# Layer 3 of a four-layer attention and feed-forward stack: when the feed-forward weights are prepared, and who copies the first turned tokens

## The chip, the core and the metric

The kernel runs on one core of a Trainium2 chip. A core has a matrix engine (TensorE, PE in the profile, with its weight loads as PEld), a vector engine (VectorE, DVE), an activation engine (ScalarE, ACT), a general engine (GpSimd, POOL) and a queue that only issues transfers (SyncE, SP). Each engine works through its own instructions in order, and waits on semaphores for the others. The metric is the device time of one execution in microseconds; lower is better.

## The reference

Four layers, each an attention block and a feed-forward block with a residual sum, on x of 4 batches x 256 tokens x 256 features, with a context of 4 x 1601 x 256. The change is in the last layer:

```python
# x = x + _L3_xattn_ref(_layernorm(x), ctx_2048, Wq, Wk, Wv)
q = x @ Wq.T
k_raw = context @ Wk.T
v_raw = context @ Wv.T
...            # 32 heads of 8 features; q and k get an rms norm over the 8
scores = jnp.einsum('bhnd,bhmd->bhnm', q, k) * scale
attn = jax.nn.softmax(scores, axis=-1)
out = jnp.einsum('bhnm,bhmd->bhnd', attn, v)

# x = x + _L3_ffn_ref(_layernorm(x), w_gate, w_up, w_down)
def _quant_weight(w):
    scale = jnp.mean(jnp.abs(w)) + EPS
    wq = jnp.clip(jnp.round(w / scale), -1.0, 1.0)
    return (wq, scale)
...            # activations are rounded to 8 bits with a scale for each token
gate = jax.nn.silu(_qlinear(x, w_gate))
up = _qlinear(x, w_up)
return _qlinear(gate * up, w_down)
```

The three feed-forward weights (each 256 x 1024 values) are thus loaded, summed in absolute value over all elements, and rounded to -1, 0 or 1 before any token can use them.

## The kernel before, in words

The kernel computes the layers one after the other; layer 3 (method `l3`) is its last fifth. Its heart is a loop of 208 **slots**: 4 batches x 4 groups of heads x 13 blocks of 128 context rows (`m`). In each slot the program issues, in this order:

- `scores`: 8 score products on TensorE (`s<-qb,kb`) into one of three PSUM tiles, and two exponentials on ScalarE (`e<-s`);
- at certain `m` a fixed extra. At the first slot of each part (`m` = 0, 3, 6, 9): the casts of the next part's keys on GpSimd (`kb<-kf`) and the loads of the part after that on SP (`kf<-kd`, 8 transfers). At `m` = 2: `close` of the group before (4 transposes, then VectorE divides). At `m` = 7: `asked`, first part (the next group's queries are split in two halves, VectorE and GpSimd). At `m` = 9: `asked`, second part: two transposes on TensorE (`b<-ident,halfq`) whose result VectorE shuffles into `row`;
- one call of `slot`, which hands out background work;
- `values` of the slot before (`o<-e,va`, 4 products). After a group's last block VectorE copies the sum out (`os<-o`), and the next group's first product into the single tile `o` has to wait for that copy. For `m` = 0 the call of `slot` comes after this.

**Background work** is written as streams: Python generators that issue some instructions and then yield. A yield of `True` means that the next piece needs TensorE and the shared PSUM tile `b`. A yield of a number is the VectorE time in microseconds that the author reckons for the next piece, 0.0 if there is next to none. `slot` serves at most one wanting stream (the one with the lowest count of pieces served for its share; none at `m` = 2 and `m` = 9), and gives every other stream at most one piece: the longest-waiting costed piece first, whatever it costs, and then others as long as they fit the room (1.7 in most slots, 1.1 at `m` = 0, 0.8 where the fixed extra took TensorE, 0.5 more if no wanting piece was served). So a yield of 0.0 is a step that holds a stream back for one slot. Nothing in this order depends on run time: all engines are pinned to program order from the first slot on (`self.strict`, lines 2353 to 2355). Because of that pinning the profile gives line L77, a helper, for nearly all instructions of the loop; they are told apart by their tiles.

The streams of batch 0 are

- `weights` (lines 2099 to 2134): for each of the three weights two loads of 512 KB on GpSimd's queue (`wf<-in_l_wg` and so on, into the two buffers of the tag `g3`), two absolute row sums on VectorE (`wsum<-wf`), one product with a matrix of ones (`b<-wsum,ones`, called here the product of the row sums), three small VectorE operations, and six rounding passes on VectorE;
- `ahead` (line 2289): mean and variance of batches 1 to 3, their inverse roots (`root3n`), and then `queries(1)`: normalised tokens (`xn`), 4 transposes into `b`, a copy to `xT`, 8 products, a copy to `qr`, squares and roots;
- `every` (line 2357, the keys) and `l3_values`: the products of the next batch's context that are still missing (`b<-wkv,ctx`, each copied out by VectorE), then from the moment that batch 1's keys have been sent those of batch 2;
- `l3_spread`: root, scaling (`kr<-kr,ss`, GpSimd), splitting (`half`, VectorE and GpSimd), turning (`kt<-half`, VectorE) and sending (`kd<-kt`, 4 transfers on SP) of batch 1's keys to memory, from where `kf` loads them.

In each later batch, `half` (line 2305) runs the feed-forward block of the batch before; it begins when all three weights are ready and the tokens are normalised (`behind`).

`bank()` is the shared PSUM tile `b`. Its pool has one buffer, so a new user waits on TensorE until the reader of the last one (mostly VectorE) has finished.

Before the loop, `queries(0)` (line 2059) runs the same steps for batch 0, without yields that matter, mixed with `fill`: products of batch 1's context (`fill<-wkv,ctx`) whose copies and squares are on ScalarE.

Of the kernel before, what the change touches and what calls it, by code (L numbers as in the profile page):

```python
# [97 lines left out]
class Kernel:  # L98
# [79 lines left out]
    def fill(self, n):  # L178

        for _ in range(n):  # L180
            next(self.early, None)
# [1828 lines left out]
    def l3(self, first):  # L2010
# [9 lines left out]
        nc, tc, i = self.nc, self.tc, self.i  # L2020
        with ExitStack() as es:
# [10 lines left out]
            def bank():  # L2032
                return ps.tile([P, 512], F32, name="b3", tag="tp")
# [9 lines left out]
            def normed(b, r):  # L2043
                xn = self.xn.tile([P, 2, D], F32, name="xn3", tag="xn")
                for q in range(2):
                    nc.vector.tensor_scalar(
                        xn[:, q, :], self.x[b][:, q, :], mv[:, b, q, 0:1], r[:, q : q + 1], ALU.subtract, ALU.mult
                    )
                return xn
# [9 lines left out]
            def queries(b, st, fill=lambda n: None):  # L2059

                xn = normed(b, rs[:, b, :])
                fill(0)
                if b:
                    yield 0.0
                yield True
                tp = bank().rearrange("p (k q t) -> p k q t", k=2, q=2)
                for k in range(2):
                    for q in range(2):  # L2070
                        self.ordered(nc.tensor.transpose(tp[:, k, q, :], xn[:, q, k * P : (k + 1) * P], self.ident))
                xT = one.tile([P, 2, S], F32, name="xT3")
                nc.vector.tensor_copy(xT, tp.rearrange("p k q t -> p k (q t)"))
                fill(1)
                yield 0.0
                yield True
                tq = bank().rearrange("p (q d) -> p q d", q=2)
                for q in range(2):
                    for k in range(2):
                        self.mm(tq[:, q, :], xT[:, k, q * P : (q + 1) * P], self.wq3[:, k, :], k == 0, k == 1)  # L2080
                qr = two.tile([P, 2, D], F32, name="qr3")
                nc.vector.tensor_copy(qr, tq)
                yield 0.8
                ss = one.tile([P, 2 * NH3], F32, name="ssq3")
                for q in range(2):
                    self.l3_squares(ss, qr[:, q : q + 1, :], q, True, two)
                yield 0.8
                if b:
                    yield from self.roots(ss, ss, 1.0 / HD3, 1e-6, two.tile([P, 1, D], F32, name="sqq3")[:, 0, :])
                    yield 0.6  # L2090
                else:
                    self.rstd(ss, ss, 1.0 / HD3, self.eps6)
                qrv = qr.rearrange("p q (h d) -> p (q h) d", d=HD3)
                nc.vector.tensor_tensor(qrv, qrv, ss[:, :, None].to_broadcast([P, 2 * NH3, HD3]), ALU.mult)
                fill(2)
                st["qr"] = qr
                yield 0.0

            def weights():

                for name, n in (("l3_wg", 2), ("l3_wu", 2), ("l3_wd", 8)):
                    v = i[name].rearrange("(k p) e -> p k e", p=P)
                    w = []
                    for c in range(2):
                        w.append(two.tile([P, I3], F32, name="wf3", tag="g3"))
                        nc.gpsimd.dma_start(
                            w[c].rearrange("p (k e) -> p k e", k=n // 2), v[:, c * n // 2 : (c + 1) * n // 2]
                        )
                    for _ in range(2):
                        yield 0.0  # L2110
                    sm = self.small.tile([P, 2], F32, name="wsum")
                    for c in range(2):
                        yield 1.2
                        nc.vector.tensor_reduce(sm[:, c : c + 1], w[c], AX.X, ALU.add, apply_absolute_value=True)
                    yield 0.0
                    yield True
                    tot = bank()[:, 0:2]
                    self.mm(tot, self.ones, sm, True, True)
                    s = one.tile([P, 1], F32, name=name + "s")
                    r = self.small.tile([P, 1], F32, name="wrec")  # L2120
                    nc.vector.tensor_reduce(s, tot, AX.X, ALU.add)
                    nc.vector.tensor_scalar(s, s, 1.0 / (I3 * D), 1e-5, ALU.mult, ALU.add)
                    nc.vector.reciprocal(r, s)
                    wb = one.tile([P, n, 2048 // n], BF16, name=name + "b")
                    wr = wb.rearrange("p k e -> p (k e)")
                    for c in range(2):
                        yield 0.8
                        nc.vector.tensor_scalar(w[c], w[c], r, RND, ALU.mult, ALU.add)
                        yield 0.7
                        nc.vector.tensor_scalar(w[c], w[c], RND, 1.0, ALU.subtract, ALU.min)  # L2130
                        yield 0.7
                        nc.vector.tensor_scalar(wr[:, c * I3 : (c + 1) * I3], w[c], -1.0, None, ALU.max)
                    wq[name], ws[name] = wb, s
                    yield 0.0
# [154 lines left out]
            def ahead(b, st):  # L2289

                if b == 1:
                    yield from norms()
                    yield 1.0
                yield from queries(b, st)
# [46 lines left out]
            for _ in queries(0, first, lambda n: [next(kv) for _ in range(FIRST3[n])]):  # L2341
                pass
# [3 lines left out]
            q = next(ask)  # L2346
# [7 lines left out]
            whole, nc = nc, InOrder(nc, self.pin)  # L2354
# [4 lines left out]
            for at, (b, g, c) in enumerate(order):  # L2359
                if g + c == 0:  # L2360
                    streams = [t for t in streams if t.left] if b else [Stream(weights(), 3)]
                    st = states[b + 1] if b + 1 < B else None
                    if b + 1 < B:
                        every.n, every.share = 0, K3[b]
                        if b == 0:
                            streams += [every, Stream(self.l3_spreads(states), 1)]
# [3 lines left out]
                k, m0 = k1, PARTS[c][0]  # L2370
                for m in range(*PARTS[c]):
# [13 lines left out]
                    if m == 7 and (g < 3 or b + 1 < B):  # L2385
# [4 lines left out]
                        q = next(ask)  # L2390
# [30 lines left out]
            def wide(dt=F32):  # L2421
                return ps_s.tile([P, 1024 if dt is F32 else 2048], dt, name="w3", tag="s3")
# [7 lines left out]
            b = B - 1  # L2430
# [6 lines left out]
            for q in range(2):  # L2437
# [8 lines left out]
                tp = wide(BF16)[:, : 2 * P].rearrange("p (k t) -> p k t", k=2)  # L2446
                for k in range(2):
                    self.ordered(nc.tensor.transpose(tp[:, k, :], vb[:, k * P : (k + 1) * P], idb))
                xT = two.tile([P, 2, P], BF16, name="xqT3")
# [217 lines left out]
```

## Time and profile before

| | |
|---|---|
| median of 3 runs | 2333.57 us |
| the runs | 2330.38, 2333.57, 2341.16 us |
| the profiled execution: its own time | 2349.27 us |
| its span, first to last instruction | 2347.5 us |
| mean granted TensorE clock in it | 0.984 |
| start of the first slot, batch 0 | 1860.43 us |
| start of slot 0 in batches 1, 2 and 3 | 1985.44, 2103.38, 2216.63 us |
| start of the last slot of batch 3 | 2315.62 us |

The profile is of one execution, which took 15.7 us more than the median of the runs. A slot is read from it as the distance between the starts of two score products (`s<-qb,kb`) on TensorE. Where nothing is late a slot takes 1.83 us without background work on TensorE (two exponentials bound it) and 2.50 us with one context product; 2.02 us with a `close`, some 3.3 us with the 8 query products. The undisturbed length is the same all through the loop, so a longer slot shows a wait or a slowed clock.

### The profile page before, as it was taken

The page shows a single profiled execution, that of the slowest core. Times are in us where ns is not written, and L with a number is a line of the kernel's source. Part 1 is how long each engine was busy: PE and PEld are TensorE (multiplying, and loading weights), DVE is VectorE, ACT ScalarE, POOL GpSimd, SP SyncE. Part 2 cuts the span into 40 slices and gives each one's busy share as a digit, 9 for nine tenths or more (in the row PEclk, how much of TensorE's full clock was granted, in tenths as well). Part 3 has the DMA queues.
Part 4 walks back from the last instruction along what each step waited for, and adds up shares of the span by engine and source line. Part 5 has one row for each costly group of instructions (what it writes and reads, how often), then busy time and mean ns, then how long its engine had stood idle before and what let it go on. Part 6 is the DMA issues. An engine that isn't in the chain of part 4 may idle for free.

```text
span 2347.5 us, 42368 instructions
## 1 busy us (share of the span) xinstructions
PE 2251.9 (96%) x14381; PEld 1381.1 (59%) x14395; DVE 1462.6 (62%) x3534; ACT 1270.3 (54%) x2884; POOL 950.3 (40%) x1723
## 2 busy tenths in 40 slices
PE   8999999889989999999999999999999989999997
PEld 5677878767745565555655555555765633343332
DVE  5553535863557777877787778877334474748343
ACT  3334445533565544455555555554332487888996
POOL 2014654513345455544555445554221253434220
PEclk9999999899999999999999999999899999999999
DMA  7165576743631111111111111100434353434220
GB/s 272 42 207 167 171 152 187 234 129 91 193 135 43 52 52 52 42 48 45 50 57 52 52 52 52 49 9 10 196 125 119 114 157 107 108 98 106 80 69 18
DMA packets 157166, 234.47 MB, mean 100 GB/s; under 512 B 33993, under 2 KB 122825, under 8 KB 155754
## 3 DMA queue, kind: packets, MB, share of 16 engines
q1 hardware_dynamic: 140902, 190.86, 25.3%
q0 software_dynamic: 11280, 31.60, 5.4%
q10 hardware_dynamic: 4772, 9.31, 1.2%
q8 instruction: 118, 1.93, 0.3%
q14 instruction: 94, 0.77, 0.1%
HBM read 169.94 MB, written 61.74 MB: 99 GB/s over the span
## 4 chain that ended last, share of the span: by engine, by line
PE 81%; DVE 8%; DMA 4%; ACT 2%; issue 2%; POOL 1%; SPq 1%; ACTq 0%; another core or an unknown queue 0%; DVEq 0%; POOLq 0%
PE o L117 18%; PE s L117 17%; PE o L77 7%; PE b L77 4%; PE f2gu L117 3%; PE s L77 3%; PE fill L1353 3%; PE acc L117 2%; PE f1gu L117 2%; PE f0gu L117 2%; PE tpq L117 2%; PE av L117 2%; PE f0y L117 2%; PE f2y L117 1%; DMA f0xr<-f0xd,f0src 1%
## 5 line engine op out<-in xcount | busy, mean ns | idle before, releaser
L1618 ACT ACTIVATE p<-s,nmsm 128x448 f32<-128x448 f32 (+2 forms) x512 | 324.3, 638 | 388.0 <-DVE nmsm L1613 316.3
L117 PE MATMUL o<-pT,va 128*128 128x256 f32 (+2 forms) x1920 | 431.6, 377 | 0.2
L117 PE MATMUL s<-kT,qT 128*32 128x448 f32 (+2 forms) x4096 | 424.2, 550 | 4.2 <-ACT p L1618 4.2
L77 ACT ACTIVATE e<-s 128x1024 f32<-128x1024 f32 (+1 forms) x416 | 393.1, 1040 | 56.3 <-PE s L77 54.3
L117 PEld LDWEIGHTS o<-pT,va 128*128 128x128 f32 (+1 forms) x1920 | 344.8, 190 | 124.3 <-issue 72.5
L1656 POOL TENSOR_SCALAR p<-p,rm 128x416 f32<-128x416 f32 x508 | 316.9, 645 | 6.3
L1613 DVE TENSOR_REDUCE nmsm<-s 128x1 f32<-128x448 f32 (+4 forms) x384 | 292.8, 783 | 4.2
L1662 DVE STREAM_TRANSPOSE pT<-p 128x448 f32<-128x448 f32 (+4 forms) x384 | 277.8, 777 | 9.7 <-POOL p L1656 9.7
L117 PEld LDWEIGHTS s<-kT,qT 128*32 128x32 f32 x4096 | 121.7, 109 | 250.2 <-issue 213.9
L77 PE MATMUL o<-e,va 128*32 128x512 f32 (+1 forms) x1664 | 249.6, 613 | 5.8 <-DVE os L77 4.1
L1646 POOL TENSOR_TENSOR rm<-em,tot 32x8 f32<-32x8 f32 x256 | 49.9, 195 | 337.1 <-DVE tot L1643 306.9
L77 PEld LDWEIGHTS s<-qb,kb 32*128 32x128 f32 (+1 forms) x1664 | 65.8, 181 | 177.2 <-issue 134.3
L1610 DVE TENSOR_TENSOR s<-s,mask 128x64 f32<-128x64 f32 (+4 forms) x384 | 92.2, 259 | 124.9 <-PE s L117 75.0
L1353 PE MATMUL fill<-wkc_early,ctxT 128*128 128x256 f32 (+1 forms) x444 | 109.6, 399 | 10.1 <-ACT va_early L1361 8.3
L545 POOL DMA_INDIRECT f0xr<-f0xd,f0src x95 | 90.9, 956 | 68.0 <-PE f0y L117 18.0
L77 PE MATMUL s<-qb,kb 32*128 32x256 f32 (+1 forms) x1664 | 111.8, 332 | 4.2 <-POOL kb L77 1.3
L1353 PEld LDWEIGHTS fill<-wkc_early,ctxT 128*128 128x128 f32 (+1 forms) x444 | 86.3, 198 | 28.0 <-ACT va_early L1361 10.4
L1618 ACT ACTIVATION_READ_ACCUMULATOR p<-s,nmsm 128x1 f32 x512 | 100.5, 196 | 0.0
L77 POOL CAST kb<-kf 128x384 fp32r<-128x384 f32 (+1 forms) x126 | 64.4, 540 | 88.2 <-PE s L77 29.8
L117 PE MATMUL f2gu<-f2wgu,f2xsT 128*128 x176 | 84.6, 605 | 0.6 <-ACT f2xsT L114 0.3
L77 PEld LDWEIGHTS o<-e,va 128*32 128x32 f32 (+1 forms) x1664 | 41.6, 108 | 68.5 <-issue 35.9
L655 POOL DMA_INDIRECT f0yt<-f0yd,f0slot x64 | 66.9, 1045 | 35.7 <-DMA kd<-kT_early 16.4
(570 smaller groups left out, 3669.1 us busy)
## 6 DMA issues: line engine op xcount, KB each, us to landing
kf<-kd SPq DMA_DIRECT2D x384, 48.0 KB
vd<-va_early SPq DMA_DIRECT2D x96, 128.0 KB
kd<-kT_early SPq DMA_DIRECT2D x48, 256.0 KB
kT<-kd SPq DMA_DIRECT2D x16, 768.0 KB
va<-vd SPq DMA_DIRECT2D x16, 768.0 KB
kd<-kt SPq DMA_DIRECT2D x96, 128.0 KB
f0yd<-f0ys SPq DMA_DIRECT2D x95, 128.0 KB
ctxT<-in_ctxT SPq DMA_DIRECT2D x5, 1664.0 KB
```

The lines of the kernel that those rows point to most:

```text
L77: ins = f(*a, **kw)
L117: self.ordered(self.nc.tensor.matmul(out, lhsT, rhs, start=start, stop=stop, **kw))
L545: nc.gpsimd.indirect_dma_start(out=t, out_offset=None, in_=xd[:, :], in_offset=bass.IndirectOffsetOnAxis(ap=src[:, n : n + 1], axis=0),)
L655: self.pin(nc.gpsimd.indirect_dma_start(out=yt, out_offset=None, in_=yd[:, :], in_offset=bass.IndirectOffsetOnAxis(ap=slot[:, t, r : r + 1 ...
L1353: ins = nc.tensor.matmul(tp[:rows, t, :], ctxT[u // NKV2][:, k, c0 : c0 + rows], w[u % NKV2][:, k, :], start=k == 0, stop=k == 1,)
L1610: nc.vector.tensor_tensor(sv, sv, mask[:, e0:e1, : nt - CT, :].rearrange("p n t i -> p n (t i)"), ALU.add)
L1613: nc.vector.tensor_reduce(ms[:, 0, e0:e1], s[:, n0:n1, : nt * 32], AX.X, ALU.max, negate=True)
L1618: nc.scalar.activation(p[:, n, : nt * 32], s[:, n, : nt * 32], AF.Exp, bias=ms[:, 0, e : e + 1], accum_out=ms[:, 1, e : e + 1],)
L1646: nc.gpsimd.tensor_tensor(r[32 * a : 32 * a + 32], e[:, a], tot, ALU.mult)
L1656: nc.gpsimd.tensor_scalar(p[:, n, : nt * 32], p[:, n, : nt * 32], r[:, e : e + 1], 1.0, ALU.mult, ALU.mult)
L1662: self.pin(nc.vector.transpose(pT[:, 2 * c + n0 : 2 * c + n1, :nt, :].rearrange("p n t i -> p n (t i)"), p[:, n0:n1, : nt * 32],))
```

## The change

Three edits, all in `l3`.

1. For batch 0 alone (`b` is 0), the copy of the turned tokens to `xT`, ahead of the loop, is issued on ScalarE (`nc.scalar.copy`) and no longer on VectorE.
2. The `weights` stream begins with twelve steps of 0.0, so its first load is issued twelve slots later.
3. Behind the two row sums of each of the three weights stand four steps of 0.0 where there was one, ahead of the piece that issues the product of the row sums.

No instruction is added or dropped; one changes its engine, and the slots of most background pieces of batches 0 to 2 change with the order.

```diff
@@ -2070,7 +2070,7 @@
                 xT = one.tile([P, 2, S], F32, name="xT3")
-                nc.vector.tensor_copy(xT, tp.rearrange("p k q t -> p k (q t)"))
+                (nc.vector.tensor_copy if b else nc.scalar.copy)(xT, tp.rearrange("p k q t -> p k (q t)"))
                 fill(1)
@@ -2098,6 +2098,8 @@
             def weights():
 
+                for _ in range(12):
+                    yield 0.0
                 for name, n in (("l3_wg", 2), ("l3_wu", 2), ("l3_wd", 8)):
@@ -2112,7 +2114,8 @@
                     for c in range(2):
                         yield 1.2
                         nc.vector.tensor_reduce(sm[:, c : c + 1], w[c], AX.X, ALU.add, apply_absolute_value=True)
-                    yield 0.0
+                    for _ in range(4):
+                        yield 0.0
                     yield True
                     tot = bank()[:, 0:2]
                     self.mm(tot, self.ones, sm, True, True)
```

## The prediction

> **What bounds the kernel now.** I read the page first (TensorE leads), then busy time and granted clock by batch of layer 3, and then the timelines of TensorE and VectorE in batch 0.
>
> ```profile
> PE 2251.9 (96%) x14381; PEld 1381.1 (59%) x14395; DVE 1462.6 (62%) x3534; ACT 1270.3 (54%) x2884; POOL 950.3 (40%) x1723
> ...
> 1860.43:1985.44 125.01, 115.18 (x931) 45.94 (x931) 79.86 (x189) 99.30 (x107) 53.46 (x81) 0.93 0.47 133
> 1985.44:2103.38 117.94, 114.52 (x1014) 47.95 (x1014) 71.09 (x185) 101.90 (x111) 46.01 (x76) 1.00 0.42 117
> ```
>
> Columns of the stretches: length, busy PE, PEld, DVE, ACT, POOL, clock, DMA share, GB/s. Batch 0 takes 125.0 us, batch 1 takes 117.9; in batch 0 TensorE is idle for 9.8 us, and only there the mean clock is under 1. The idle time stands in a few stops:
>
> ```profile
> 1852.04 1.99 PE L117 MATMUL b<-wq,xT 128*128 128x256 f32 x8 [2.09 <-DVE xT L2073]
> ...
> 1895.20 1.27 PE L77 MATMUL o<-e,va 128*32 128x512 f32 x8 [2.57 <-DVE os L77]
> ...
> 1914.33 0.38 PE L77 MATMUL b<-wsum,ones 128*128 128x2 f32 x2 [2.90 <-DVE wsum L77]
> ...
> 1942.63 0.89 PE L77 MATMUL s<-qb,kb 32*128 32x256 f32 x8 [1.34 <-POOL kb L77]
> ```
>
> And behind the three in the loop the clock is low for 3.4 us:
>
> ```profile
> 1896.40:1899.80 3.40, 3.40 (x28) 1.50 (x24) 2.33 (x7) 1.94 (x2) 3.04 (x4) 0.57 0.84 200
> ...
> 1916.90:1920.30 3.40, 3.40 (x26) 0.91 (x24) 3.26 (x11) 1.76 (x3) 2.58 (x4) 0.57 0.31 87
> ...
> 1944.20:1947.60 3.40, 3.40 (x19) 1.45 (x17) 0.77 (x3) 2.13 (x3) 0.00 (x0) 0.57 0.35 99
> ```
>
> The first two stops have one cause: VectorE is some 4 us late all through slots 7 to 30. It copies a group's sum out late (`os`), and the row sums of the second weight stand behind other work and a transfer:
>
> ```profile
> 1887.25 0.44 DVE L77 STREAM_SHUFFLE row<-b 128x256 f32<-128x256 f32 x1
> ...
> 1894.47 0.68 DVE L77 COPY os<-o 128x512 f32<-128x512 f32 x1
> ...
> 1908.80 1.22 DVE L77 TENSOR_REDUCE wsum<-wf 128x1 f32<-128x1024 f32 x1 [0.94 <-DMA wf<-in_l_wu]
> 1936.49 1.22 DVE L77 TENSOR_REDUCE wsum<-wf 128x1 f32<-128x1024 f32 x1 [2.35 <-DMA wf<-in_l_wd]
> ```
>
> The `row` of slot 9 comes at 1887.25, though its transposes ended at 1883.3. The third stop is the same lateness passed on: SP sends turned keys only after VectorE has turned them, key loads queue behind those sends, and the casts (`kb`) wait for them.
>
> **The order after.** The slot rule fixes the order of both versions. Stepping the streams through it gives, for before, each of the trace's 208 slots with the TensorE work that it shows. The slots in which pieces are issued (batch 0 unless said):
>
> - first weight: load 0 → 12, sums 3, 5 → 15, 17, product 7 → 23, last rounding 14 → 29
> - second: load 15 → 30, sums 18, 19 → 33, 34, product 21 → 39, last rounding 27 → 47
> - third: load 28 → 48, sums 31, 33 → 51 and slot 0 of batch 1, product 45 → slot 16 of batch 1, last rounding slot 0 → 23 of batch 1
> - queries of batch 1: `xn` 11 → 8, transposes and `xT` copy 13 → 10, products 16 → 12
> - keys of batch 1: sends 10..33 → 8..28; context products of batch 2: 36..51 → 30..45
> - feed-forward of batch 0: 12..48 → 25..51 of batch 1. Batch 3 keeps its order.
>
> No slot is added, and TensorE's and ScalarE's totals stay (but for the one copy). The later products of the row sums hold back only the roundings and through them batch 0's feed-forward block, which now ends in slot 51 of batch 1; nothing waits for its result, so that costs nothing as long as its TensorE pieces find slots, which they do. What moves is lateness.
>
> **What goes.** Slot lengths less the undisturbed 1.83, 2.50 and 2.02: slots 14 and 15 (4.28, 3.32, the latter with a `close`) 2.45 + 1.30; slots 21 and 22 (4.72, 3.28) 2.89 + 1.45; slots 34, 35, 36 (3.25, 3.29, 3.01, the last with a product) 1.42 + 1.46 + 0.51; slot 49 (3.46 with a product, behind `row`) 0.96. Sum 12.4 us. Each stop costs its idle time and about 1.3 to 2 us of low clock. They go if VectorE is on time at these places. Its work in slots 13 to 19 after is 1.4, 2.5, 2.1, 3.2, 2.5, 2.2 and 1.1 us (from the rows: a row sum 1.21, a turn 1.24, a root step 1 to 1.7, a rounding pass 0.7 to 0.9), about 3 us late at slot 18, worked off by slot 23. In that time TensorE waits for VectorE only through `row` at slot 22, whose splitting is issued at slot 20, and for the product at slot 23, six slots behind its second sum. So I take all 12.4.
>
> **What comes.** (a) Slot 9's transposes leave their result in `b`, and slot 10 now wants `b` for the queries' transposes; before, four slots lay between. VectorE up to that `row` loses the two row sums (1.21 + 1.19), three small operations (0.46) and a rounding pass (0.74), 3.6 us, and gains the last root steps (0.7), one split (0.45) and `xn` (1.70), 2.9 us. So `row` ends near 1887.4 against 1888.0. TensorE stands at the transposes of slot 10 from 1884.8 (the slot's start 1884.31 + 0.44 of scores): 2.6 us, less 0.3 for a late start of slots 9 and 10 themselves, is a new stop of 2.3 us, plus 1.3 of clock: 3.6. Bounds: 1.0 (under the 1.15 us stop at 1992, behind which the clock stayed 1.00) and 4.34 (slots 21 and 22). What is queued behind: this batch's `o` and the next scores; ScalarE runs dry with them. The `os` of slot 13 then finds VectorE on time.
>
> (b) The loads. Rows: the second weight's sum began 6.5 us after its load's issue, the third's 5.3, both on landing. First weight: three slots from load to sum, one of 3.3 us, no stop. Second: three slots with products, 7.5 us; none. Third: issued behind slot 48's casts, some 2.4 us into it; lands at 7.7 where VectorE asks at 6.5; then one split, and `os` of the next slot at about 9.35 where the sum is ready at 8.8 and `o` wanted at 9.6. That is the 0.35 to 0.45 us wait that `os` has elsewhere. Cost 0; bounds -0.5 and 3.75 (slots 14 and 15). GpSimd's casts behind the loads have three slots of room; SP issues as many transfers as before.
>
> The Trainium skill (DMA: Bandwidth & Descriptors, Anatomy of one DMA) reckons 2.0 us plus bytes over 436 GB/s, an estimate of 3.2 us for 512 KB. The rows of 5.3 and 6.5 us, with the queue shared, decide; by the page (b) could not cost anything.
>
> (c) Batches 1 and 2: the feed-forward block meets root and split of batch 3's keys in slots 44 to 50 of batch 1; VectorE has 3.3 + 3.1 + 2.9 us in three slots of 2.5, 2.5 and 1.98, 2.6 us late at most; `b` is wanted at once after `row` in slot 49. I take +0.5; bounds 0 and 2.5. The long slot 22 of batch 2 (2.82) has another order: -0.5, bounds -1 and 0.
>
> (d) The `xT` copy. VectorE's copy ran 1851.30 to 1851.98, behind a reduction that waited for a ScalarE square until 1850.66. On ScalarE it follows the pair of copies that ends near 1851.1; 128x256 copies there take 0.37, so 128x512 about 0.65, done near 1851.7: -0.3. Bounds: -1.9 (first in line, at 1849.5) and +0.9 (behind the next pair and square).
>
> Sum: -12.4 + 3.6 + 0 + 0.5 - 0.5 - 0.3 = -9.1 us, on a span of 2347.5; the median is 0.6% shorter, which changes the sum by 0.1. Forecast 2324.5.
>
> A rule against this: the Trainium skill (TensorE: Matmul & The Clock Gate, HAM oscillation) asks only that no idle gap exceed about 3.4 us. By it the stops of 2.57, 2.90 and 1.34 cost no clock. The 0.57 behind each of them says otherwise here; by the rule 4.7 us of the 12.4 (1.30 + 1.45 + 1.46 + 0.51) and 1.3 of the 3.6 would not be there: -5.7.
>
> **Rivals.** *A, the stop at slot 10 is short.* For it: without a GpSimd operation beside them, root steps take 0.17 us (they took 1.0 to 1.28 with one). Against: `kr` and `half` run there after too. With 1.0 for (a) the sum is -11.7, with (d) at its best -13.3: 2320 to 2322.
>
> *B, the lateness only changes places.* (a) at 4.34, (b) at 3.75, (c) at 2.5 and 0, (d) as forecast: -2.1, 2331.5. Against: by the same sum of VectorE's work it is at most 1.7 us late in slots 23 to 50.
>
> *C, slower: the row sums stand on their loads.* VectorE waits in order; a sum that waits for its load holds `row`, the copies out of `b` and `os` behind it. The bound from the trace is the first weight's load, issued at 1862.2 beside the 1.7 MB context loads and used unhindered at 1872.8: at most 10.6 us. At 10.6 in all three places: first 3.9 (2.6 at slot 22 and the clock), second 0.5, third 6.6 (5.3 at `os` and the clock): +11.0, net +1.9, 2335.5. From some 9.9 us it is slower than before. Against: the two rows at 5.3 and 6.5.
>
> **How the numbers follow.** Two medians of this kernel differ without a change by up to about 0.5% (the three runs spread 10.8 us); 0.5% is 2321.9 or less, or 2345.2 or more. Forecast 0.51 (own range 2319.5 to 2330), A 0.23, B 0.10, C 0.10, and 0.06 for a slowdown that none of these names. Faster by over 0.5%: 0.42 of the forecast's share, for its 9.1 lies 2.6 short of the bound with that spread, and 0.83 of A: 0.41. Slower: half of C (where loads take longer still) and the unnamed: 0.11. The rest, 0.48, is within. Range 2316 to 2336: A's best and the runs' spread below, C at the top.
>
> **What would show it.** Right: no stop behind `os` at slot 14 nor behind `wsum`; batch 0 near 116 us; one stop of about 2 us at the transposes `b<-ident,xn` in slot 10, its releaser `row` on VectorE, and low clock behind it; `kb` never the releaser of a stop. Wrong: no stop there (A), `wsum` waiting for its load by over 3 us (C), or new stops of over 1.3 us in batch 1 (B).

## The result, and the profile after

The changed kernel took 2346.80 us (median of 6 runs, 2342.53 to 2349.07), the kernel before 2337.17 us beside it (6 runs, 2330.38 to 2341.16). The ratio is 1.0044, with a 95% interval of 1.0032 to 1.0055: slower by some 10 us, where 9 us less were forecast.

The profiled execution of the kernel after took 2343.73 us, that of the kernel before 2349.27 us. The two spans thus say the opposite of the medians. The loop of layer 3 does not: from its first score product to that of its last slot it went from 455.19 to 462.63 us. First the page's busy times, then the stretches of the loop's first three batches, in the columns of the prediction (length, busy PE, PEld, DVE, ACT, POOL, granted clock, DMA share, GB/s):

```profile
PE 2246.1 (96%) x14395; PEld 1379.0 (59%) x14395; DVE 1462.4 (62%) x3533; ACT 1277.2 (55%) x2885; POOL 948.2 (40%) x1723
```

```profile
1847.16:1971.69 124.53, 112.22 (x928) 44.16 (x928) 80.59 (x189) 98.82 (x107) 58.50 (x87) 0.95 0.51 140
1971.69:2097.95 126.26, 119.57 (x1026) 50.09 (x1024) 79.68 (x202) 102.91 (x111) 45.32 (x75) 0.97 0.41 106
2097.95:2210.80 112.85, 110.44 (x980) 43.68 (x976) 55.86 (x160) 100.40 (x111) 36.94 (x67) 1.00 0.37 90
```

Busy time does not show the loss; the totals are those of before. Batch 0 did not fall to 116 us but stayed at 124.5 (before: 125.0), and batch 1 grew from 117.9 to 126.3, with a clock under 1 that it did not have before. The timeline of TensorE (start, length, line, output<-inputs, idle time before and what ended it) shows where:

```profile
1871.86 0.63 PE L77 MATMUL b<-ident,xn 128*128 128x128 f32 x4 [1.94 <-DVE row L77]
...
1896.93 0.39 PE L77 MATMUL s<-qb,kb 32*128 32x256 f32 x4 [1.42 <-POOL kb L77]
...
1900.75 0.69 PE L77 MATMUL b<-ident,halfq 128*128 128x128 f32 x2 [2.72 <-POOL halfq L77]
...
1963.50 0.69 PE L77 MATMUL b<-ident,halfq 128*128 128x128 f32 x2 [1.94 <-POOL halfq L77]
...
1977.68 1.94 PE L77 MATMUL o<-e,va 128*32 128x512 f32 x8 [3.68 <-DVE os L77]
```

The first is the forecast stop of slot 10. The old stops at `os` (slot 14), `wsum` (slot 21) and `kb` (slot 34) are gone, as forecast. The other rows are new: slot 22, slot 48, and slot 1 of batch 1. The stop of slot 22 has its chain in VectorE and GpSimd. VectorE first (the turn of slot 14, the first weight's two row sums, the last root step of the keys' second part):

```profile
1884.47 1.25 DVE L77 STREAM_TRANSPOSE kt<-half 128x1024 f32<-128x1024 f32 x1 [2.45 <-DMA kf<-kd]
...
1887.70 1.21 DVE L77 TENSOR_REDUCE wsum<-wf 128x1 f32<-128x1024 f32 x1
...
1891.45 1.21 DVE L77 TENSOR_REDUCE wsum<-wf 128x1 f32<-128x1024 f32 x1
...
1894.90 0.33 DVE L77 SCALAR_TENSOR_TENSOR ss<-half 128x160 f32<-128x160 f32 x1
```

Then GpSimd, which waits for that last step:

```profile
1895.31 1.07 POOL L77 TENSOR_TENSOR kr<-kr,ss 128x512 f32<-128x512 f32 x1 [5.88 <-DVE ss L77]
1896.32 1.26 POOL L77 CAST kb<-kf 128x449 fp32r<-128x449 f32 x2
1897.54 1.70 POOL L77 TENSOR_TENSOR half<-kr,half 128x512 f32<-128x512 f32 x1
1899.21 1.07 POOL L77 TENSOR_TENSOR kr<-kr,ss 128x512 f32<-128x512 f32 x1
1900.24 0.45 POOL L77 TENSOR_TENSOR halfq<-qr,halfq 128x128 f32<-128x128 f32 x1
```

Slot 18 began at 1888.11; the scaling issued in it began 7.2 us later, and everything behind it on GpSimd, the casts `kb` and the queries' `halfq` that TensorE needs in slot 22, is late with it. In slot 48 VectorE waited for GpSimd's squares of keys (`sq`), and a rounding pass of the second weight came before the queries' split, which GpSimd's `halfq` needs:

```profile
1961.49 0.69 DVE L77 TENSOR_REDUCE ss<-sq 128x64 f32<-128x512 f32 x1 [4.10 <-POOL sq L77]
1962.10 0.68 DVE L77 TENSOR_SCALAR wf<-wf 128x1024 f32<-128x1024 f32 x1
1962.70 0.22 DVE L77 TENSOR_SCALAR halfq<-qr 128x128 uint32<-128x128 uint32 x1
```

At the start of batch 1 the same two engines stand in the way of `os`:

```profile
1973.65 1.25 DVE L77 STREAM_TRANSPOSE kt<-half 128x1024 f32<-128x1024 f32 x1 [3.94 <-POOL half L77]
1975.47 1.22 DVE L77 TENSOR_REDUCE wsum<-wf 128x1 f32<-128x1024 f32 x1 [0.58 <-DMA wf<-in_l_wd]
1976.61 0.42 DVE L77 TENSOR_SCALAR half<-kr 128x512 uint32<-128x512 uint32 x1
1976.94 0.68 DVE L77 COPY os<-o 128x512 f32<-128x512 f32 x1
```

TensorE stood from 1974.0 us on (1977.68 less 3.68); a turn that waited 3.94 us for GpSimd and a row sum of the third weight were ahead of `os` in VectorE's queue. VectorE's part of that split was done at 1969.7 us. GpSimd was late with its part (`half`) because two casts, until 1970.7, and then the third weight's load issue stood ahead of it:

```profile
1970.71 1.60 POOL L77 DMA_DIRECT2D wf<-in_l_wd  x2
1972.33 1.29 POOL L77 TENSOR_TENSOR half<-kr,half 128x512 f32<-128x512 f32 x1
```

### The profile page after: what moved, and what is told of

It is laid out like the page before. It is cut to its first block, busy times and chain, and to the rows that moved or that the text cites. A ratio compares the mean times of both kernels' runs of the same rounds, so it can differ in the third digit from the quotient of the medians.

```text
span 2341.9 us, 42389 instructions
## 1 busy us (share of the span) xinstructions
PE 2246.1 (96%) x14395; PEld 1379.0 (59%) x14395; DVE 1462.4 (62%) x3533; ACT 1277.2 (55%) x2885; POOL 948.2 (40%) x1723
## 3 DMA queue, kind: packets, MB, share of 16 engines
q8 instruction: 118, 1.93, 0.3%
## 4 chain that ended last, share of the span: by engine, by line
PE 78%; DVE 8%; DMA 5%; ACT 3%; issue 3%; POOL 2%; SPq 1%; ACTq 0%; POOLq 0%; DVEq 0%
PE o L117 18%; PE s L117 17%; PE o L77 7%; PE b L77 3%; PE f2gu L117 3%; PE s L77 3%; PE acc L117 2%; PE f0gu L117 2%; PE f1gu L117 2%; PE tpq L117 2%; PE av L117 2%; PE fill L1353 2%; PE s L329 2%; DMA f0xr<-f0xd,f0src 2%; PE f0y L117 1%
## 5 line engine op out<-in xcount | busy, mean ns | idle before, releaser
L117 PEld LDWEIGHTS o<-pT,va 128*128 128x128 f32 (+1 forms) x1920 | 344.8, 190 | 124.5 <-issue 72.5
L77 PE MATMUL s<-qb,kb 32*128 32x256 f32 (+1 forms) x1664 | 112.9, 333 | 4.4 <-POOL kb L77 1.7
L117 PE MATMUL f0gu<-f0w,f0xsT 128*128 x380 | 78.0, 327 | 1.6 <-DVE ss_early L126 1.2
```

The lines of the kernel that those rows point to most:

```text
L77: ins = f(*a, **kw)
L117: self.ordered(self.nc.tensor.matmul(out, lhsT, rhs, start=start, stop=stop, **kw))
```

## The experiments

The runs were made on several occasions, on which the kernel before had medians from 2334 to 2348 us, so each version is compared with runs of the kernel before beside it. The ratio is the one given with the result; it need not be exactly the quotient of the medians. As a second, finer measure I give the loop **from slot 4 of batch 0 to the last slot** in the profile: the first four slots differ by some 2 us between executions of one kernel, and the part ahead of the loop by over 10. Before: 442.88 us. After: 452.46 us.

### Are the profiles typical? (e5, e14)

The kernel before and the changed kernel, each profiled a second time, nothing changed.

> The kernel before, profiled a second time. Theory chance (the prediction's terms were read from one execution that stood 13 us above the median of its own kernel): the stretch from the first fill product to the first score is 22.65 us without the 2.09 us stop before the query products, and the loop of layer 3 (first score to last) is 451 to 453 us instead of 455.2. Theory structure (the stops belong to the kernel): 25.0 us and 455 us again.

> The changed kernel again, beside the two others on one chip, with a second profile. If its stops belong to the kernel: os 3.5 to 3.9 us at the start of batch 1, halfq 2.5 to 2.9 in slot 22, loop 461 to 465, time 8 to 12 us above the kernel before. If they were the chance of one execution: loop under 458, time within 5 us.

Before: 2332.17 us in its one run (2334.14 beside it); the 22.65 us from the first fill product to the first score have no stop at the query products; loop 449.69, from slot 4 439.53. TensorE's stops in it, and batch 0:

```profile
1880.62 1.06 PE L77 MATMUL o<-e,va 128*32 128x512 f32 x8 [2.66 <-DVE os L77]
1898.71 0.38 PE L77 MATMUL b<-wsum,ones 128*128 128x2 f32 x2 [1.85 <-DVE wsum L77]
1926.01 0.89 PE L77 MATMUL s<-qb,kb 32*128 32x256 f32 x8 [0.61 <-POOL kb L77]
```

```profile
1847.89:1967.32 119.43, 111.02 (x932) 44.07 (x932) 81.54 (x189) 99.29 (x107) 53.90 (x81) 0.97 0.50 140
```

The places are the same, but the stops at `wsum` and `kb` are smaller (2.90 and 1.34 us in the first profile), and the 2.09 us stop ahead of the query products is not there. So the first profile of before, 16 us above the median of the first three runs, was dearer than the kernel: 3.4 us of it in the loop from slot 4, 2.1 in the first four slots, 2.4 between the first fill product and the first score, and the rest ahead of that. The theory of chance holds, and by more than it said.

After, again: 2359.12 us against 2347.21, ratio 1.0053 (1.0034 to 1.0073); from slot 4 452.20 us (first profile 452.46); slot 22 stops 1.26 and 2.72 us, the start of batch 1 4.82 (3.5 to 3.9 were expected). The stops of after belong to the kernel.

Slot lengths above the undisturbed ones given with the profile before (a slot with the four query transposes is taken at 2.1 us), in both profiles of each (us):

| slots | before | after | the prediction's term |
|---|---|---|---|
| batch 0, 9 to 11 | 0.0, 0.0 | 2.0, 2.0 | +3.6 (a) |
| 14 to 16 | 3.8, 3.9 | 0.7, 0.7 | -3.8 |
| 21 to 25 | 4.6, 3.2 | 7.6, 7.0 | -4.3 |
| 34 to 36 | 3.4, 1.1 | 0.4, 1.4 | -3.4 |
| 48 and 49 | 0.9, 0.9 | 3.1, 1.6 | -1.0 |
| batch 1, 1 to 3 | 1.5, 1.5 | 6.1, 6.9 | 0 (b) |
| 46 to 48 | 0.0, 0.0 | 2.9, 2.9 | +0.5 (c) |
| batch 2, 1 to 4 and 22 | 1.9, 1.9 | 1.7, 1.7 | -0.5 (c) |

These places add up to 8.4 us more in the first pair of profiles and 11.7 in the second, of the 9.6 and 12.7 us by which the loop from slot 4 grew.

### The parts of the change one by one (e1, e2, e3)

```diff
-                nc.vector.tensor_copy(xT, ...)                                   # e1 alone
+                (nc.vector.tensor_copy if b else nc.scalar.copy)(xT, ...)
+                for _ in range(12):                                              # e2 alone
+                    yield 0.0
-                    yield 0.0                                                    # e3 alone
+                    for _ in range(4):
+                        yield 0.0
```

> Kernel before with the first edit alone (xT copied by ScalarE for batch 0). The trace of after has 22.65 us from the first fill product to the first score, before has 25.01. If the copy alone does that, this kernel has no stop before the 8 query products and is 2 to 2.5 us faster than before (0.1%), with the loop's stops where before has them. Rival: the 2.4 us came with the other edits or by chance; then no gain, and the first stop stays at 2.09 us.

> Kernel before with the second edit alone (twelve steps ahead of the weights). Theory G (GpSimd's queue): the key scaling of batch 1's second part is still issued at slot 18 and 19, ahead of the queries' subtraction of slot 20, and so holds it; a stop at the transposes of slot 22 as in after (2 to 3 us, 6 to 8 with clock and neighbours), another in slot 48, but no row sum ahead of the copy out of o at the start of batch 1. Against before: 0 to +6 us. Theory W (the weights come too late for batch 1): most of the loss of after, +8 or more, with stops in batch 1. Theory L (loads collide with the sends of keys): a load at slots 12, 26 and 40 beside sends, stops behind turns that wait for landing sends, +5.

> Kernel before with the third edit alone (four steps behind the row sums). Theory G: the key scaling falls behind the subtraction (slot 21 after slot 20, slot 47 after slot 46), so GpSimd does not hold it; the product of the second weight's row sums stands six slots behind its sum, so the stop of 2.90 us at wsum goes; the query transposes stand at slot 12, three slots behind the last user of b, and their stop is under 1 us. Faster than before by 4 to 10 us. Theory W: also later weights, so slower, +2 to +5. Theory L: loads at slots 0, 19 and 36, the second beside a send, gain at most 3.

| | median, us | before | ratio | loop from slot 4 |
|---|---|---|---|---|
| e1, copy | 2336.51 | 2335.77 | 1.0005 (0.9995 to 1.0015) | 440.41 |
| e2, 12 steps | 2341.34 | 2335.77 | 1.0033 (1.0021 to 1.0046) | 447.47 |
| e3, 4 steps | 2340.92 | 2335.77 | 1.0027 (1.0014 to 1.0039) | 449.71 |

The copy shows no gain in the time, and each of the two others costs 5 to 6 us by itself (6 to 8 by the ratios). The whole change costs about as much as both, but the stops are not the same ones, so it is no sum of parts. Twelve steps alone (e2) bring the stops that after has in slots 10 and 22 (1.93 and 3.09 us), the latter as theory G said, and others in slots 19, 34 and 47 (1.57, 2.67 and 1.39). Four steps alone (e3) leave slot 22 without a stop, as theory G said, but stop in slots 10, 27 and 38 (2.83, 1.58 and 1.90 us): slower by 5 us where theory G had 4 to 10 us of gain.

In e3 a stop at `os` comes at the start of batch 1 (3.50 us), and in e2 and e3 at the start of batch 2 (2.51 and 2.53 us). In all three places the steps of the streams put a turn into the last slot of the group, so that it stands ahead of `os` on VectorE, and ahead of the turn VectorE waits 2.7 to 2.8 us for GpSimd's squares.

The copy can be seen only in executions that have the stop ahead of the query products. There the stop was 1.35 to 2.09 us with the copy on VectorE (before, e11, e15) and 0.37 to 1.71 us with it on ScalarE (e9, e10, e12, e13, e14); the rows below are of e11 and e10, further down. From the first fill product to the first score these executions took 24.95 to 25.00 us with VectorE's copy and 24.56 to 24.77 with ScalarE's. All others have no such stop and took 22.65 us, whichever engine copied.

```profile
1844.97 1.99 PE L117 MATMUL b<-wq,xT 128*128 128x256 f32 x8 [2.04 <-DVE xT L2073]
```

```profile
1854.53 1.99 PE L117 MATMUL b<-wq,xT 128*128 128x256 f32 x8 [1.71 <-ACT xT L2073]
```

### Remedies at single places (e4, e6, e7, e8, e9)

All five are the changed kernel with one more edit: e4, the subtraction for `halfq` on VectorE; e6, the first weight's load at slot 0 again, its sums where they were; e7, the subtraction of every split ahead of a turn on VectorE; e8, the `os` of the start of batch 1 on ScalarE; e9, the third weight eight steps later.

```diff
-        nc.gpsimd.tensor_tensor(tv[:, :, :, 1, :], vv, tv[:, :, :, 0, :], ALU.subtract)
+        (eng or nc.gpsimd).tensor_tensor(...)     # e4: eng=nc.vector from asked; e7: from l3_spread
-                for _ in range(12):               # e6: these 12 steps stand behind the load
-                    yield 0.0
-                    for _ in range(2):
+                    for _ in range(14 if name == "l3_wg" else 2):
-                            nc.vector.tensor_copy(os, last[1])                       # e8
+                            (nc.scalar.copy if last[3] == 3 and not last[5] else nc.vector.tensor_copy)(os, last[1])
+                    for _ in range(8 if name == "l3_wd" else 0):                     # e9
+                        yield 0.0
```

> Kernel after, with the subtraction of the queries' halves (asked) on VectorE instead of GpSimd. Theory G: the stops at the transposes of slots 22 (2.72 us) and 48 (1.94 us) that wait for halfq on GpSimd lose most of their length, and the low clock behind them; the stop for kb at slot 22 (1.42) stays, and the copy out of o in batch 1 (3.68) comes 2 to 3 us less late. 6 to 10 us faster than after. Theories W and L: the transposes then wait as long for VectorE, within 2 us of after.

> The changed kernel, with the first weight's load alone issued at slot 0 again; its row sums and everything behind them stay at the slots of the changed kernel. Theory L (the 512 KB pair of loads at 1876 us delays the landing of the turned keys' sends, so that the turn of slot 14 waits 2.45 us and all of VectorE's and GpSimd's work behind it is late): the stops at kb 1.42 and halfq 2.72 of slot 22 shrink to under 1.5 together, the loop is 3 to 6 us shorter than the 462.6 of the changed kernel, the time 3 to 6 us below it. Theory G (the order of the work in the queues of VectorE and GpSimd alone sets the stops): within 1 us of the changed kernel.

> The changed kernel with the subtraction of every split ahead of a turn on VectorE in place of GpSimd, in layer 3's loop. Theory G (VectorE and GpSimd wait for one another in turn, each in its own order, and what TensorE needs, os and halfq, stands behind these waits): the os stop of 3.68 us at the start of batch 1 falls below 1 us, the halfq stops of 2.72 and 1.94 us shrink, loop 453 to 458 instead of 462.6, time 5 to 9 us below the changed kernel. Rival V (VectorE has too much work at these places, and 0.7 us more per split makes it later still): time 0 to 5 us above the changed kernel, os stop 3 us or more.

> The changed kernel with the one copy of o to os at the start of batch 1 on ScalarE in place of VectorE. Theory G (os is late only because it stands behind a turn that waits 3.94 us for GpSimd): the 3.68 us stop goes, slots 1 and 2 of batch 1 lose 5 of their 5.85 us of excess, ScalarE pays 0.7: loop 457.5 to 459, time 4 to 5.5 us below the changed kernel. Rival (VectorE is late whatever is taken from it, and the close of the next slot meets it): a stop of 1.5 us or more stands at the transposes or products behind the close, and the time falls by less than 2.5 us.

> The changed kernel with the third weight alone loaded eight steps later (load in slot 4, row sums in slots 7 and 9 of batch 1; the product of the row sums stays in slot 16). Theory W (at the start of batch 1 os is late because the third weight's load issue, 1.60 us on GpSimd, stands ahead of the split that the turn waits for, and its row sums ahead of os): slots 1 and 2 of batch 1 keep less than 1.5 of their 5.85 us of excess, batch 1 takes 119 to 122 us instead of 126.3. A turn then falls into slot 51 of batch 1, right ahead of os, so up to 4 us may come at the start of batch 2: time 1 to 5 us below the changed kernel. Rival T (the turn waits for the split whatever the weight does): the os stop stays at 2.5 us or more and the time within 1.5 us of the changed kernel.

| | median, us | before | ratio | loop from slot 4 | batch 1 |
|---|---|---|---|---|---|
| after | 2346.80 | 2337.17 | 1.0044 (1.0032 to 1.0055) | 452.46 | 126.26 |
| e4 | 2350.08 | 2335.77 | 1.0062 (1.0049 to 1.0075) | 454.03 | 125.39 |
| e6 | 2343.24 | 2334.14 | 1.0035 (1.0023 to 1.0048) | 450.19 | 125.70 |
| e7 | 2344.92 | 2334.14 | 1.0040 (1.0026 to 1.0055) | 449.29 | 127.70 |
| e8 | 2346.55 | 2334.14 | 1.0045 (1.0032 to 1.0058) | 453.07 | 127.75 |
| e9 | 2357.04 | 2347.67 | 1.0051 (1.0032 to 1.0071) | 452.24 | 122.79 |

None gives more than some 3 us, by the loop or by the ratio; all five gains that were expected were missed. The traces say why. In e4 `halfq` no longer stands in GpSimd's queue, and slot 22 stops nearly as long for VectorE (and slot 34, with 1.39 us at most in after, for 4.26):

```profile
1906.21 0.44 PE L77 MATMUL b<-ident,halfq 128*128 128x128 f32 x2 [2.46 <-DVE halfq L77]
```

In e8 the stop at `os` falls to 0.89 us, and the next two things that TensorE wants are late instead:

```profile
1982.26 1.07 PE L77 MATMUL o<-e,va 128*32 128x512 f32 x8 [0.89 <-ACT os L77]
1987.33 0.84 PE L77 MATMUL s<-qb,kb 32*128 32x256 f32 x8 [1.99 <-POOL kb L77]
1990.62 1.08 PE L77 MATMUL b<-ident,xn 128*128 128x128 f32 x4 [2.44 <-DVE t L77]
```

In e7 the turn ahead of `os` waits for nothing any more, and still TensorE stops for `os` (3.89 us), for VectorE now has one piece behind the other ahead of it:

```profile
1969.58 1.45 DVE L77 TENSOR_TENSOR half<-kr,half 128x512 f32<-128x512 f32 x1
1971.06 1.25 DVE L77 STREAM_TRANSPOSE kt<-half 128x1024 f32<-128x1024 f32 x1
1972.25 1.22 DVE L77 TENSOR_REDUCE wsum<-wf 128x1 f32<-128x1024 f32 x1
1973.39 0.42 DVE L77 TENSOR_SCALAR half<-kr 128x512 uint32<-128x512 uint32 x1
1973.84 0.69 DVE L77 TENSOR_TENSOR half<-kr,half 128x512 f32<-128x512 f32 x1
1974.45 0.68 DVE L77 COPY os<-o 128x512 f32<-128x512 f32 x1
```

In e9 that stop falls from 3.68 to 1.59 us and batch 1 by 3.5 us, but the turns have moved with it, and batch 2 takes 116.39 us instead of 112.85. In e6 the `kb` stop of slot 22 goes (1.42 us) and the `halfq` stop stays (2.52): where the load stands, with its issue and its traffic, is some 2 us of the loop, not the main cause.

So it is not one instruction in the wrong queue. The pair VectorE and GpSimd is late at these places (TensorE's stops in after are 1.3 to 4.8 us long), and in these runs the next need of TensorE met what one remedy had saved.

### Taking the weights out of these places (e10, e12, e13), and two counter-tests (e11, e15)

e10 and e12 change only the two numbers of the change: 24 steps and 4, 25 and 3. e13 is e12 with the subtraction of e7. e15 is the kernel before with that subtraction alone. e11 is the kernel before, where a turn is not issued in a group's last slot:

```diff
-                    if t is now or t.want or not t.left or not (first or t.cost <= room):
+                    if t is now or t.want or not t.left or not (first or t.cost <= room) or t.cost == held:
...
-                        slot(streams, free, room)
+                        slot(streams, free, room, 1.25 if m == NM - 1 else None)
```

> The changed kernel with 24 steps of delay in place of 12: the first weight's load and row sums move from slots 12 to 17 to slots 24 to 28, while root, split and asked of slots 14 to 22 stay. Theory C (slot 22 stops because the first weight's load and two row sums, 2.4 us, are put into a stretch of VectorE that the split and two roots fill already): the stops of slot 22 (kb 1.42, halfq 2.72) shrink to under 1.5 us together, slots 21 to 25 keep under 2 of their 7.9 us of excess, batch 0 takes 117 to 120 us. The start of batch 1 is open: the second weight's sums now lie in slots 43 and 45. Time 4 to 8 us below the changed kernel if nothing comes new there. Rival R (the two roots and the key scaling ahead of halfq suffice for the stop): 2.5 us or more remain in slot 22, time within 2 us of the changed kernel.

> The kernel before, with one rule added: a turn is not issued in the last slot of a group, so that it comes behind os and not ahead of it (slot 12 to 13 of batch 0, slot 25 to 26 of batch 1; the second and third weight move by two slots or fewer). Theory O (os is late where VectorE meets, just ahead of it, an instruction that waits for GpSimd): the os stop of 2.7 us in slot 14 falls under 0.6, slots 14 and 15 lose 2.5 to 3.5 us, loop 446 to 448 against 449.7 and 455.2 in the two profiles of the kernel before, time 2 to 4 us below it. Rival P (VectorE is late whatever its order, and the next wait of TensorE takes the place of this one): the os stop goes, but 2 us or more come up in slots 15 to 22; time within 1 us.

> The changed kernel with 25 steps of delay and three steps behind the sums in place of 12 and four: the first weight's two row sums stand in slots 28 and 29, behind the close of slot 28 instead of ahead of it (with 24 steps a stop of 2.23 us stood there); at the start of batch 1 neither a load nor a row sum nor a turn stands just ahead of os. Theory C (collisions of the weights' row sums and load issues with the split, asked, close and os set the time, not the number of steps as such): the 2.23 us stop goes, loop 446 to 449 (2 us more where the first two slots meet the low clock), time 2 to 4 us below the kernel before and 9 to 13 below the changed kernel run beside it. Rival P (what is saved in one place comes up in another): within 1.5 us of the kernel before.

> The same with 25 and three steps, and the subtraction of every split ahead of a turn on VectorE. Theory G (VectorE and GpSimd waiting for one another in turn is what remains): 1 to 4 us below the version without it, the stops at halfq of slots 22 and 48 under 1 us. Rival V (VectorE's work is what remains): 0 to 3 us above it, with stops of 2 us or more at row in slot 10 and at kr near slot 34.

> The kernel before, with nothing changed but the subtraction of every split ahead of a turn, on VectorE in place of GpSimd. If the gain of 0.24% of the version with 25 steps came from this subtraction alone (theory H): 4 to 7 us below the kernel before, and the delay of the weights is worth nothing in any form. If it needs both (theory C: with the weights begun at slot 0 their load, row sums and roundings still meet the split in slots 3 to 33, and VectorE gets 0.7 us more per split there): within 2 us of the kernel before or slower, with an os stop of 1.5 us or more in slot 14 or a wsum stop in slots 21 to 23.

| | median, us | before | ratio | loop from slot 4 | batches 0 (from slot 4), 1, 2 |
|---|---|---|---|---|---|
| before, two profiles | | | | 442.88, 439.53 | 112.7, 117.9, 113.3; 109.3, 118.0, 113.3 |
| e10 | 2346.11 | 2347.67 | 0.9994 (0.9981 to 1.0006) | 437.56 | 107.4, 117.3, 113.9 |
| e12 | 2346.51 | 2347.21 | 0.9993 (0.9979 to 1.0007) | 436.87 | 106.3, 117.8, 113.9 |
| e13 | 2341.27 | 2347.21 | 0.9976 (0.9963 to 0.9989) | 433.60 | 103.1, 116.2, 115.3 |
| e14, after again | 2359.12 | 2347.21 | 1.0053 (1.0034 to 1.0073) | 452.20 | 113.4, 126.9, 112.9 |
| e11 | 2348.51 | 2347.67 | 1.0013 (0.9999 to 1.0027) | 442.29 | 112.0, 118.0, 113.3 |
| e15 | 2350.93 | 2347.99 | 1.0008 (0.9996 to 1.0020) | 446.16 | 112.2, 121.2, 113.7 |

With 24 steps the first weight's load and sums leave slots 12 to 17, while root, split and `asked` stay where they were. The key scaling of slot 18 then begins 3.3 us after the slot (7.2 in after), and what is left of slot 22's two stops is the first row below. The second is a new stop, for which the profile names no releaser:

```profile
1915.63 0.44 PE L77 MATMUL b<-ident,halfq 128*128 128x128 f32 x2 [1.60 <-POOL halfq L77]
...
1930.81 1.10 PE L77 MATMUL b<-wkv,ctx 128*128 128x256 f32 x4 [2.23 <-issue]
```

Ahead of it, on VectorE, a turn waited 3.41 us for a transfer, and then a row sum of 1.18 us stood before the divides of a `close`, which read the tile `b` that the stopped product needs. With 25 and 3 steps the sum stands behind the `close`, and 1.11 us are left of the stop. At the start of batch 1, where no load, sum or turn now stands directly ahead of `os`, its stop is 0.72 us instead of 3.68 and 4.82. Against the changed kernel on the same occasion (e14), e12 is 12.6 us faster and e13 17.9. **e13 beats both kernels**: 0.24% below the kernel before, with an interval of 0.11 to 0.37%. The loops of e10 and e12, 2 to 6 us shorter than those of before, are of one execution each, and the times of these two versions do not bear them out. The first two batches of e13 beside those of after on the same occasion (e13 first, then e14):

```profile
1860.26:1975.62 115.36, 110.01 (x928) 44.24 (x928) 83.31 (x198) 98.42 (x107) 48.38 (x76) 0.97 0.53 152
1975.62:2091.83 116.21, 113.89 (x1000) 47.31 (x1003) 77.50 (x199) 102.17 (x111) 34.13 (x63) 1.00 0.41 110
```

```profile
1857.67:1983.42 125.75, 113.04 (x929) 44.98 (x930) 80.34 (x189) 99.02 (x107) 56.94 (x85) 0.95 0.48 137
1983.42:2110.34 126.92, 118.50 (x1018) 50.00 (x1022) 79.56 (x202) 102.80 (x111) 46.67 (x77) 0.97 0.39 106
```

VectorE has no less to do in these two batches (83 + 78 us against 80 + 80), GpSimd 21 us less. What went are waits: behind its first two slots e13's loop has two stops of over 0.6 us (2.10 in slot 10, 1.29 in slot 24 of batch 2), while those of e12 in slots 22, 29 and 48 (1.56, 1.11, 1.18) and at the start of batch 1 (0.72 and 1.44) are gone. So theory G of e13 was right, and its gain larger than expected: 5.2 us below e12 by the medians, and eleven of its twelve runs (2344.26 us at most) are faster than eleven of e12's (2344.57 at least). The subtraction alone shows no gain (e15), and 25 steps alone none that can be measured: it takes both. In e11 the turn was moved from ahead of `os`, and the saving came back as a longer stop in slot 23:

```profile
1887.26 1.06 PE L77 MATMUL o<-e,va 128*32 128x512 f32 x8 [1.68 <-DVE os L77]
1911.04 0.56 PE L77 MATMUL b<-wsum,ones 128*128 128x2 f32 x2 [3.59 <-DVE row L77]
```

No run keeps 12 and 4 steps and only starts batch 2's keys later. So how much of slot 48 and of the start of batch 1 is due to the earlier squares and splits of those keys stays open.

## Why the prediction was wrong

The step that failed is in **What goes**: "about 3 us late at slot 18, worked off by slot 23. In that time TensorE waits for VectorE only through `row` at slot 22, whose splitting is issued at slot 20", from which followed "So I take all 12.4"; and in (b) in "GpSimd's casts behind the loads have three slots of room". The order of the pieces was right: the three products of the row sums, for one, came in slots 23, 39 and 16 of batch 1.

- VectorE ended slot 18's last root step at 1895.2, 5.3 us after that slot's end, where 3 were summed: the durations were right, but the wait of the turn of slot 14, 2.45 us, was left out. And I looked only for what TensorE takes from VectorE directly. The way is longer: VectorE's last root step, GpSimd's key scaling, the casts, a split, a second scaling, and only then `halfq`. Slots 21 to 25 keep 7.0 to 7.6 us of excess where 0 was forecast. e10, which takes the load and the sums out of slots 12 to 17, brings them to 1.5.
- **(b)** was put at 0, bounds -0.5 and 3.75. It was 4.6 to 5.4 us. I had reckoned with the load's landing (0.58 us of wait, where the sum had 1.2) and one split ahead of `os`. But I had the load issued "some 2.4 us into" slot 48; GpSimd was so late that it issued it 9.7 us into it (1970.71, the slot began at 1961.05). And the issue, 1.60 us on GpSimd ahead of the split that the turn waits for, was not in the sum. In e9, without the third weight's load and sums there, 1.59 us of the 3.68 us stop stay.
- A new stop in slot 48 was in no term: with VectorE's wait of 4.10 us for GpSimd's squares ahead of the queries' split, slots 48 and 49 became 0.7 to 2.2 us longer than before. **(c)** was +0.5 and -0.5: slots 46 to 48 of batch 1 cost 2.9, just above the upper bound of 2.5; batch 2 came out 0.2 below before.
- **(a)** was right in place, releaser and length: 1.94 us with `row` as its releaser against 2.3 forecast. The added 1.3 us of low clock did not come (1.00 behind the stop), so 2.0 instead of 3.6. That is luck of the execution: behind the stop of slot 10 in e4, e7, e8 and e9 (1.94 to 2.47 us) the clock was 0.52 to 0.58 over 3.4 us.
- The stops that were to go did go from slots 14 and 34, but in the second profile of after slot 34 has another one, of 1.39 us. And the 12.4 us were read from one execution; in the second profile of the kernel before these places hold about 9 us. I had noted that the median stood 0.6% below the profiled span, and scaled the sum by 0.6% instead of asking which of the stops made the difference.
- **(d)** was -0.3. Where an execution has the stop, the stretch to the first score fell by 0.2 to 0.4 us, as forecast; where it has none, by nothing. In the time it does not show: e1 is within 0.15% of the kernel before.

Of the rivals, B had the mechanism (the lateness changes places) and priced it at -2.1 us, with the argument against it drawn from the same sum. The result is worse than B above all by what none of the cases held: slot 22 and slot 48. C did not happen: of the row sums ahead of a stop only one waited for its load, for 0.58 us.

## What to carry to other kernels

When two in-order engines feed one another, sum the chain through both queues, with the waits, and follow it to every piece that the bounding engine takes, also from the engine that you did not touch; a remedy at one piece (e4, e8, e11) handed the wait to the next here. What helped was to take work out of the stretch in which both are already full, and to shorten the way between the two; look first at what stands just ahead of each copy that TensorE needs at once. And before pricing stops from one profile, profile the unchanged kernel twice: some 3.4 of the 12.4 us here were that execution's.

## What the runs showed of the hardware

The granted clock behind a stop does not follow from the stop's length alone. Three stretches of 3.40 us of the kernel after, in the columns of the batches, each from the end of a stop on (slots 10, 22, 48):

```profile
1871.86:1875.26 3.40, 3.40 (x34) 1.30 (x36) 2.00 (x4) 1.34 (x3) 3.04 (x7) 1.00 0.71 167
1900.75:1904.15 3.40, 3.40 (x19) 1.18 (x20) 2.35 (x6) 0.02 (x1) 3.01 (x6) 0.50 0.74 168
1963.50:1966.90 3.40, 3.40 (x22) 1.18 (x26) 2.85 (x8) 0.19 (x2) 0.81 (x2) 0.50 0.12 28
```

The first and third stops are both 1.94 us; behind the one the clock is full, behind the other half. The traces show what goes with it. In layer 3's loop, in all 17 profiles, the stretches of half clock begin whole multiples of 3.413 us apart within an execution and last 3.41, 6.83 or 10.24 us; in after they begin at 1898.66, 1963.51 and 1977.17. On this grid the third stop (1961.56 to 1963.50) lies wholly in one interval (1960.10 to 1963.51), and the first (1869.92 to 1871.86) is cut at 1871.35, 1.43 us before and 0.51 behind. All 29 intervals of full clock in which TensorE stood idle for more than 1.80 us were followed by half clock; of those with less some were (from 0.76 us on) and most were not. So where a stop falls on the grid bears on its price; an exact rule does not come out of these runs.

An operation of VectorE with two SBUF inputs stretched beside GpSimd: in e7 the subtraction that began at 1969.58 took 1.45 us while GpSimd scaled keys (from 1969.20, for 1.28 us), and the same operation took 0.69 us four microseconds later, with GpSimd idle. One with a single input stretched too: VectorE's part of that split took 1.32 us from 1968.23 on, while GpSimd issued a load until 1969.18, and 0.42 us at 1973.39. The Trainium skill (SBUF — State Buffer, "SBUF: two separate sides") says that the two engines share a pair of ports, which one of them locks for a whole instruction. The two rows of the subtraction agree with it; that the lock was held in them no run here shows.

In some executions of either kernel ScalarE pauses for 2.3 to 3.5 us shortly ahead of the query products (2.96 us in e10), and these are the ones with the stop there; the others have neither. Apart from the first profile of before it goes with the occasion: all of e9 to e15 have it, beside which the kernel before took 2347 to 2348 us, and after and e1 to e8 do not, beside which it took 2334 to 2337 us. Why was not found.
